# Smaller last chunks and a new place for the last value sums in a sparse graph-attention kernel

## Chip, core and metric

The kernel runs on one core of a Trainium2 chip. The metric is device time in microseconds (us) of one execution; lower is better. The engines are TensorE (PE in the profile), VectorE (DVE), ScalarE (ACT), GpSimd (POOL) and SyncE (SP).

## What is computed

The input is a matrix `x` of 3327 nodes with 256 features and an adjacency matrix with about 16 neighbours in each row. Layer 0 is a small graph attention; layers 1 to 3 are transformer layers whose attention is masked by the adjacency matrix:

```python
def layer(x, adj, ...):                      # layers 1, 2 and 3, 8 heads of 32
    q, k, v = split(layer_norm(x, g1, be1) @ w_qkv)
    scores = einsum('nhd,mhd->hnm', q, k) * HEAD_DIM ** -0.5
    attn = softmax(where(adj != 0, scores, -inf))
    x = x + einsum('hnm,mhd->nhd', attn, v) @ w_proj + b_proj
    h2 = layer_norm(x, g2, be2)
    return x + gelu(h2 @ w1 + b1) @ w2 + b2  # 256 -> 1024 -> 256
```

## The kernel before

Layer 0 also builds, for each node, the list of its neighbours. The nodes are sorted by their number of neighbours and cut into 26 blocks of 128. Block `b` has room for `CAPS[b]` neighbours: 40 for block 0, 24 for block 1, falling to 10 for block 25. Each of the layers 1 to 3 then works on gathered rows in place of a dense matrix.

**Groups.** The neighbours of a block are taken four at a time (`GS = 4`). A group is one tile `kv` with up to four rows of k and v for each of 128 nodes. It is filled by one indirect DMA for each neighbour, issued on GpSimd (L1226); ten such tiles are in a ring (`NBUF = 10`), and `issue()` for the next tile stands behind the step that frees one. There are 121 groups and 448 gathers in a layer.

**The order.** `ORDER` takes the blocks as 25, 1, 24, 2, ..., 14, 12, 13, and last block 0, the longest, with ten groups. In what follows K(b, s) is `scores` on the group of block `b` that starts at neighbour `s`: a product and a sum over each head on VectorE (L1248, L1249). V(b, s) is `values` on the same group: a product on VectorE (L1289, into one of three `vw` buffers) and two matmuls by the identity on TensorE, which the chip runs as four instructions (L1294), summed in the PSUM bank `po`. V follows K of the same block by roughly a block, since it needs the softmax.

**A turn.** `run()` goes through the groups in order. In each turn it does one K, then up to two V from `todo`, and then `some()`. A block's V may start when `wait` of the block is over 1, that is two turns after its last K. Two V are done in a turn when over five wait in `todo`, or when the block is block 0.

**Short steps.** After its last V a block puts nine steps on the list `short` (of which three are empty): copy and fold of `po`, a transpose (L1319), a copy, the projection (L1328, L1330), and `add` (L1334), which also takes the statistics of the second layer norm. `some()` takes one at its start and one at its end.

**Chunks and long steps.** Blocks are put together in chunks, by `CHUNK`: 3, 4, 4, 4, 4, 4, 2 and 1 blocks. When the last block of a chunk has been added, the chunk's steps are put on the list `long`: normalization (`scale`, 13 small VectorE instructions), transposes (L591), eight `up` matmul groups (L1373) with `gelu` on ScalarE (L1379), eight `down` groups (L1396, or L1389 for one block), the way back (L1402, L1410), the additions (L1414). In layers 1 and 2 there follow a second `scale`, transposes, and for each block `qkv` (L1426) and `keep` (L1432 to L1434), which writes the block's k and v rows for the next layer. In layer 3 there follows one `store` for each block (L1439), an indirect DMA on GpSimd. The next layer's first gather needs all `keep` writes of the layer.

**Pace.** Each long step has a cost. `some()` adds `rate` to `credit`, which is held to at most 8, and takes long steps while `credit` is over 0. For a chunk of four blocks the costs sum to 73.5 in layers 1 and 2, where two cost units of `up` or `down` are four matmul instructions with 512 columns. The rate is that sum over the number of groups in the next four blocks less two, about 16 turns, so 4.59. For the last chunk it is the sum over five.

**The end of a layer.** After the last K the remaining V are done one by one with `some()` in between, then `rate` is 4 and both lists are emptied.

The order within each engine is the order in which the program is written; the scheduler does not move instructions. So a step that waits holds up all that stands behind it on its engine.

Of the kernel before, what the change touches and what calls it, by code (L numbers as in the profile page):

```python
# [32 lines left out]
NB = (N + P - 1) // P  # L33
# [25 lines left out]
NBUF = 10  # L59

CB = 4
# [462 lines left out]
def sparse_path(ctx, tc, ins, out, dram, flag):  # L524
# [98 lines left out]
    with tc.tile_pool(name="a", bufs=1) as a, tc.tile_pool(name="aw", bufs=2) as aw, \  # L623
# [391 lines left out]
        def some(n):  # L1015
            for _ in range(n):
                if late:
                    late.pop(0)()
# [14 lines left out]
        for i in range(NB):  # L1033
# [8 lines left out]
            k = 1 if i < NB - 2 else 2  # L1042
# [147 lines left out]

    ORDER = [b for k in range(NB // 2) for b in (NB - 1 - k, k + 1)][:NB - 1] + [0]
    CHUNK, at = {}, 0
    for n in [CB - 1] + [CB] * ((NB - CB - 2) // CB) + [2, 1]:
        for b in ORDER[at:at + n]:
            CHUNK[b] = ORDER[at:at + n]
        at += n
    assert at == NB
    slots = {b: [(b, s) for s in range(0, CAPS[b], GS)] for b in ORDER}

    class Layer:  # L1200
# [101 lines left out]
        def block(self, b):  # L1302
            L, w, c = self.L, self.w, {}
            x = t2[:, b, :D]
            chunk = CHUNK[b]
            if b == chunk[0]:
                self.n2 = Norm(len(chunk), f"f{L}_{b}")
            n2 = self.n2

            def copy():  # L1310
                c["o"] = work.tile([P, D], FP, tag="o", name=f"o_{L}_{b}")
                nc.scalar.copy(c["o"], self.po[b][:, :D])

            def fold():
                nc.vector.tensor_add(c["o"], c["o"], self.po[b][:, D:])

            def turn():
                for k in range(2):
                    nc.tensor.transpose(self.po[b][:, k * P:(k + 1) * P],  # L1319
                                        c["o"][:, k * P:(k + 1) * P], ident)  # L1320

            def copy_T():
                c["oT"] = work.tile([P, 2 * P], FP, tag="oT", name=f"oT_{L}_{b}")
                nc.scalar.copy(c["oT"], self.po[b][:, :2 * P])

            def project():
                ps = self.po[b][:, D:]
                nc.tensor.matmul(ps, ones_bf[:96, :], bias3[:, 0, :], start=True, stop=False)  # L1328
                for k in range(2):
                    nc.tensor.matmul(ps, c["oT"][:, k * P:(k + 1) * P], w["w_proj"][:, k, :],  # L1330
                                     start=False, stop=(k == 1))

            def add():
                nc.vector.tensor_add(x, x, self.po.pop(b)[:, D:])  # L1334
                n2.stats(chunk.index(b), x)
                if b == chunk[-1]:
                    self.long += self.chunk(chunk, n2)
                    at = ORDER.index(b) + 1
                    turns = sum(len(slots[i]) for i in ORDER[at:at + CB])
                    turns = 5 if at == NB - 1 else turns - 2  # L1340
                    self.rate = sum(cost for cost, _ in self.long) / max(turns, 1)

            return [lambda: None, copy, lambda: None, fold, turn, copy_T, project, lambda: None, add]

# [133 lines left out]
        def some(self):  # L1478

            if self.short:  # L1480
                self.short.pop(0)()
            self.credit = min(self.credit + self.rate, 8.0)
            while self.long and self.credit > 0:
                cost, step = self.long.pop(0)
                self.credit -= cost
                step()
            if self.short:
                self.short.pop(0)()

        def run(self):  # L1490
            for _ in range(NBUF):
                self.issue()
            self.take_q(ORDER[0])

            todo, wait = [], {}

            def value():
                if todo[0][1] == 0:
                    self.weights(todo[0][0])
                self.values(*todo.pop(0))  # L1500

            for k, b in enumerate(ORDER):
                for g in slots[b]:
                    self.scores(*g)
                    if g == slots[b][-1]:
                        self.softmax(b)
                        if k + 1 < NB:
                            self.take_q(ORDER[k + 1])
                    for i in wait:
                        wait[i] += 1  # L1510
                    for _ in range(2 if len(todo) > NBUF // 2 or b == 0 else 1):
                        if todo and wait[todo[0][0]] > 1:
                            value()
                    self.some()
                todo += slots[b]
                wait[b] = 0
            while todo:
                value()
                self.some()
            self.rate = 4.0  # L1520
            while self.short or self.long:
                self.some()
# [45 lines left out]
```

## Time and profile before

| | |
|---|---|
| median of 10 runs | 2890.05 us (2876.18 to 2895.62) |
| the profiled execution | 2893.88 us |
| its span, first to last instruction | 2892.1 us |
| PE busy | 2005.4 us (69%) |
| DVE busy | 1981.1 us (69%) |
| POOL busy | 1359.2 us (47%) |
| ACT busy | 792.0 us (27%) |
| first gather of layers 1, 2, 3 | 634.2, 1414.7, 2187.5 us |
| last gather ends, layers 1, 2, 3 | 1293.2, 2067.5, 2797.0 us |

How to read it: busy shares are means over stages that differ. In each of the three layers there is a stretch with gathers (about 660, 653 and 610 us) and an end without (121 us from the last gather of layer 1 to the first of layer 2, 120 us from layer 2 to 3, and 95 us to the end of the span).

### The profile page before, as it was taken

The page shows a single profiled execution, that of the slowest core. Times are in us where ns is not written, and L with a number is a line of the kernel's source. Part 1 is how long each engine was busy: PE and PEld are TensorE (multiplying, and loading weights), DVE is VectorE, ACT ScalarE, POOL GpSimd, SP SyncE. Part 2 cuts the span into 40 slices and gives each one's busy share as a digit, 9 for nine tenths or more (in the row PEclk, how much of TensorE's full clock was granted, in tenths as well). Part 3 has the DMA queues.
Part 4 walks back from the last instruction along what each step waited for, and adds up shares of the span by engine and source line. Part 5 has one row for each costly group of instructions (what it writes and reads, how often), then busy time and mean ns, then how long its engine had stood idle before and what let it go on. Part 6 is the DMA issues. An engine that isn't in the chain of part 4 may idle for free. (4 is left out here: it accounts for less than half of the span.)

```text
span 2892.1 us, 21905 instructions
## 1 busy us (share of the span) xinstructions
PE 2005.4 (69%) x6391; PEld 1062.7 (37%) x6391; DVE 1981.1 (69%) x4141; ACT 792.0 (27%) x1363; POOL 1359.2 (47%) x1461
## 2 busy tenths in 40 slices
PE   4566666623778887787347878978782588777866
PEld 4444444411334333344213434434351243333334
DVE  2977787457787787773378876776724886778852
ACT  2443443200223332332102322322231023222221
POOL 3000000027775665650377656655405777777740
PEclk9677666756888988898678988988986799889988
DMA  4323321137776766660477656655506766666650
GB/s 178 135 97 113 125 105 55 50 116 218 217 222 186 203 203 181 187 179 16 138 209 210 194 176 176 193 168 153 135 26 184 210 201 195 188 190 189 204 136 15
DMA packets 144479, 453.67 MB, mean 157 GB/s; under 512 B 29521, under 2 KB 40156, under 8 KB 141021
## 3 DMA queue, kind: packets, MB, share of 16 engines
q0 software_dynamic: 113056, 370.26, 44.7%
q1 hardware_dynamic: 9834, 53.90, 5.2%
q10 hardware_dynamic: 21458, 28.02, 2.7%
q8 instruction: 52, 0.85, 0.1%
q14 instruction: 79, 0.65, 0.1%
HBM read 420.64 MB, written 31.42 MB: 156 GB/s over the span
## 5 line engine op out<-in xcount | busy, mean ns | idle before, releaser
L1226 POOL DMA_INDIRECT kv<-kv,t x1344 | 1273.3, 947 | 814.2 <-issue 355.4
L1294 PE MATMUL po<-vw,s_ident 128*128 128x512 f32 (+1 forms) x1380 | 773.1, 696 | 498.0 <-DVE vw L1289 450.1
L1248 DVE TENSOR_TENSOR kv<-kv,q 128x1024 f32<-128x1024 f32 (+3 forms) x363 | 413.2, 1138 | 311.0 <-ACT q L1234 153.6
L1294 PEld LDWEIGHTS po<-vw,s_ident 128*128 128x128 f32 x1380 | 284.7, 220 | 847.9 <-issue 470.8
L1249 DVE TENSOR_REDUCE sc<-kv 128x32 f32<-128x1024 f32 (+3 forms) x363 | 414.1, 1141 | 12.5
L1289 DVE TENSOR_TENSOR vw<-kv,w 128x1024 f32<-128x1024 f32 x333 | 371.2, 1127 | 0.2
L1373 PE MATMUL pu<-fT,s_w 128*128 128x512 f32 (+3 forms) x768 | 304.8, 531 | 1.0 <-ACT fT L596 1.0
L1396 PE MATMUL py<-gT,s_w 128*128 128x512 f32 (+2 forms) x672 | 282.9, 548 | 0.0
L1379 ACT ACTIVATE gT<-pu,pvb 128x512 f32<-128x512 f32 (+3 forms) x192 | 116.5, 608 | 355.6 <-PE pu L1373 355.3
L702 POOL MEMSET s_abf<- 128x1 bf16 x26 | 2.6, 103 | 434.9 <-PE s_ptb L714 252.0
L1373 PEld LDWEIGHTS pu<-fT,s_w 128*128 128x128 f32 x768 | 148.9, 203 | 138.6 <-issue 113.9
L1396 PEld LDWEIGHTS py<-gT,s_w 128*128 128x128 f32 x672 | 127.2, 191 | 122.3 <-issue 104.6
L714 PE MATMUL s_ptb<-s_ident_bf,s_abf 128*128 128x128 bf16 x676 | 76.6, 292 | 114.4 <-ACT s_aT L715 83.2
L724 DVE MAX8 cand<-s_v 128x8 f32<-128x208 bf16 x416 | 117.5, 359 | 0.9
L1426 PE MATMUL pk<-s_w_qkv,nT 128*128 128x512 f32 x208 | 110.1, 655 | 8.5 <-ACT nT L596 8.5
L714 PEld LDWEIGHTS <-s_abf 128*128 128x128 bf16 x676 | 65.4, 135 | 127.6 <-issue 93.5
L588 ACT ACTIVATE xn_f<-t,nm_f,rqy_f 128x256 f32<-128x256 f32 x78 | 42.9, 593 | 247.1 <-DVE nm_f L582 239.9
L1334 DVE TENSOR_TENSOR t<-t,po 128x256 f32<-128x256 f32 x78 | 32.5, 417 | 107.9 <-PE po L1330 104.0
L1263 ACT ACTIVATE sc<-sc,mx 128x120 f32<-128x120 f32 (+6 forms) x78 | 32.0, 410 | 259.5 <-DVE mx L1260 258.9
L715 ACT COPY s_aT<-s_ptb 128x896 bf16<-128x896 bf16 x104 | 83.3, 853 | 65.8 <-PE s_ptb L714 65.8
L1186 POOL DMA_INDIRECT t<-t,perm x26 | 24.6, 947 | 157.4 <-DMA colsb<-in_L_gnn_be_dram 149.8
L1414 DVE TENSOR_TENSOR t<-t,pd 128x256 f32<-128x256 f32 x75 | 29.5, 408 | 93.4 <-PE pd L1410 93.4
(285 smaller groups left out, 2458.3 us busy)
## 6 DMA issues: line engine op xcount, KB each, us to landing
s_a<-in_adj_dram SPq DMA_DIRECT2D x25, 1663.5 KB
kv<-kv,t POOLq DMA_INDIRECT x1344, 3.7
kv<-kvr ACTq DMA_DIRECT2D x52, 256.0 KB
kv<-s_kvr ACTq DMA_DIRECT2D x26, 256.0 KB
s_w<-in_L_gnn_w_dram SPq DMA_DIRECT2D x6, 1024.0 KB
t<-ql ACTq DMA_DIRECT2D x6, 592.0 KB
t<-s_x ACTq DMA_DIRECT2D x6, 512.0 KB
s_w_qkv<-in_L_gnn_w_qkv_dram SPq DMA_DIRECT2D x3, 768.0 KB
```

Of the source, the lines that this page charges most:

```text
L714: nc.tensor.transpose(pt[:, m, :], self.abf[:, k * P:(k + 1) * P], ident_bf)
L715: nc.scalar.copy(aT[:, k0:k0 + len(ks), :], pt[:, :len(ks), :])
L724: nc.vector.max(out=self.cand[:, s, :], in_=v[:, s, :])
L1226: nc.gpsimd.indirect_dma_start(out=t[:, s, :], out_offset=None, in_=kv[L], in_offset=bass.IndirectOffsetOnAxis(ap=t2[:, b, k:k + 1].bitcas ...
L1248: nc.vector.tensor_mul(k, k, self.q[b][:, None, :].to_broadcast([P, n, D]))
L1249: nc.vector.tensor_reduce(self.sc[b][:, s0:s0 + n, :], k.rearrange("p s (h d) -> p s h d", d=HD), AX.X, ALU.add)
L1289: nc.vector.tensor_mul(vw[:, :n * D].rearrange("p (s h d) -> p s h d", h=HEADS, d=HD), v, self.wp[b][:, s0:s0 + n, :, None].to_broadcast([ ...
L1294: nc.tensor.matmul(self.po[b][:, :m], ident, vw[:, s * D:s * D + m], start=(s0 + s == 0), stop=(s0 + s + 2 >= S), skip_group_check=True)
L1373: nc.tensor.matmul(c["pu", f][:, :n], w["w1"][:, e, f * P:(f + 1) * P], c["hT"][:, e, :n], start=(e == 0), stop=(e == 1))
L1379: nc.scalar.activation(g[:, :n], c.pop(("pu", f))[:, :n], AF.Gelu_apprx_tanh, bias=w["b1"][:, f:f + 1])
L1396: nc.tensor.matmul(c["py"][e][:, :n], w["w2"][:, f, e * P:(e + 1) * P], g[:, :n], start=(f == 0), stop=last)
L1426: nc.tensor.matmul(ps[:, :c1 - c0], c["hT"][:, e, j * P:(j + 1) * P], nxt["w_qkv"][:, e, c0:c1], start=(e == 0), stop=(e == 1))
```

## The change

Four edits, all in `CHUNK` and in the methods of `Layer`:

1. The chunks are 3, 4, 4, 4, 4, 2, 2, 2 and 1 blocks: blocks 10, 15, 11, 14, which were one chunk of four, become [10, 15] and [11, 14].
2. The rate is the sum of the waiting costs over 12 for a chunk of three or four blocks, and over 5 for a smaller one.
3. `some()` takes two short steps at its end instead of one when over eight wait, that is, right after a block's last V.
4. In the last two blocks of `ORDER` (13 and 0) two V are done in each turn and a block's V may start as soon as its softmax has been written; and after the last K all ten V of block 0 are done in one go, without `some()` in between.

```diff
-    for n in [CB - 1] + [CB] * ((NB - CB - 2) // CB) + [2, 1]:
+    for n in [CB - 1] + [CB] * 4 + [2, 2, 2, 1]:
...
-                    at = ORDER.index(b) + 1
-                    turns = sum(len(slots[i]) for i in ORDER[at:at + CB])
-                    turns = 5 if at == NB - 1 else turns - 2
-                    self.rate = sum(cost for cost, _ in self.long) / max(turns, 1)
+                    self.rate = sum(cost for cost, _ in self.long) / (12 if len(chunk) > 2 else 5)
...
-            if self.short:
-                self.short.pop(0)()
+            for _ in range(2 if len(self.short) > 8 else 1):
+                if self.short:
+                    self.short.pop(0)()
...
-                    for _ in range(2 if len(todo) > NBUF // 2 or b == 0 else 1):
-                        if todo and wait[todo[0][0]] > 1:
+                    last = k >= NB - 2
+                    for _ in range(2 if len(todo) > NBUF // 2 or last else 1):
+                        if todo and wait[todo[0][0]] > (not last):
                             value()
                     self.some()
...
             while todo:
                 value()
-                self.some()
```

## Prediction

> **What bounds the kernel now.** I read the busy time by stages first, since shares of the whole span hide that the stages differ. The columns are the stretch, its length, then busy us of PE, weight loads, DVE, ACT and POOL, the granted TensorE clock, the DMA share and GB/s. The first four rows go from K(11,0) of layer 1 to its last softmax and on to layer 2's first gather, and then the end of layer 3:
>
> ```profile
> 1149.00:1255.00 106.00, 86.23 (x216) 40.67 (x215) 76.71 (x135) 32.65 (x69) 64.07 (x69) 0.87 0.64 184
> 1255.00:1308.00 53.00, 45.57 (x117) 20.94 (x117) 39.18 (x63) 15.96 (x34) 29.07 (x31) 0.97 0.67 165
> 1308.00:1415.00 107.00, 74.05 (x249) 45.96 (x249) 31.49 (x104) 27.30 (x56) 0.34 (x1) 0.84 0.14 47
> ...
> 2806.00:2892.00 86.00, 55.94 (x192) 35.30 (x192) 25.39 (x64) 16.39 (x33) 7.07 (x7) 0.83 0.03 12
> ```
>
> Each layer ends with 86 to 107 us without gathers, in which TensorE works two thirds of the time. Next, one full cycle of a four-block chunk in the middle of layer 2 (turns K(9,4) to K(11,4), 103 us), cut at its stages: the FFN, then additions and second norm, then qkv:
>
> ```profile
> 1832.60:1877.50 44.90, 44.35 (x116) 20.76 (x115) 30.21 (x42) 19.54 (x29) 32.13 (x35) 0.97 0.68 200
> 1877.50:1897.90 20.40, 9.66 (x24) 3.93 (x22) 17.99 (x40) 2.56 (x5) 8.11 (x9) 0.73 0.44 130
> 1897.90:1911.80 13.90, 13.15 (x31) 6.97 (x32) 5.47 (x12) 4.64 (x8) 6.62 (x7) 0.66 0.52 152
> ```
>
> The bound alternates. In the FFN TensorE is never free and VectorE loses 44.9 - 30.2 = 14.7 us; in the additions VectorE is nearly full and TensorE idles; in qkv VectorE loses 8.4. Together they are the 23 us in which each cycle exceeds VectorE's own work.
>
> Layer 3 is another case. Its POOL rows show gathers back to back, 1.25 us apart, broken only by pairs of stores:
>
> ```profile
> 2558.39 0.94 POOL L1226 DMA_INDIRECT kv<-kv,t  x1 [0.30 <-issue]
> 2559.64 1.00 POOL L1439 DMA_INDIRECT out_dram<-t,perm  x1 [0.30 <-issue]
> 2563.26 0.98 POOL L1439 DMA_INDIRECT out_dram<-t,perm  x1 [2.62 <-DVE vw L1289]
> 2564.55 0.99 POOL L1226 DMA_INDIRECT kv<-kv,t  x1 [0.30 <-issue]
> ```
>
> 448 gathers x 1.25 = 560 of the 610 us from 2187.5 to 2797.0; a pair of stores adds 4.9 (2559.64 to 2564.55) in place of nothing. So layer 3's middle ends with GpSimd. The chain of waits of its last stretch:
>
> ```profile
> 2851.95 8.85 PE po L1294 x16
> 2861.22 0.43 DVE o L1315
> 2861.70 0.45 PE po L1319 x2
> 2862.87 0.88 PE po L1330 x4
> 2863.84 0.43 DVE t L1334
> ```
>
> The last V of block 0 end at 2860.8, 52 us after its softmax (2808.6), though ten V are 17.2 us of TensorE: chunk steps stand between them. From block 0's `add` (2863.85) to the end are 28.2 us, a chain with one block that the change leaves as it is.
>
> Prices on TensorE, from rows in order of time:
>
> ```profile
> 1852.60 1.88 PE L1373 MATMUL pu<-fT,s_w 128*128 128x512 f32 x4
> 1854.32 1.88 PE L1396 MATMUL py<-gT,s_w 128*128 128x512 f32 x4
> ```
> ```profile
> 1890.31 3.66 PE L1294 MATMUL po<-vw,s_ident 128*128 128x512 f32 x4 [4.79 <-DVE vw L1289]
> ```
> ```profile
> 2834.77 1.03 PE L1373 MATMUL pu<-fT,s_w 128*128 128x256 f32 x4
> 2835.63 1.03 PE L1396 MATMUL py<-gT,s_w 128*128 128x256 f32 x4
> ```
>
> Four instructions with 512 columns take 1.72 us (1852.60 to 1854.32), with 256 columns 0.86, and after an idle time of 4.8 us 3.66: a cold TensorE costs 1.9 more.
>
> **Layer 3's end.** Block 0's gathers end one store pair later, since [10, 15] now stores ahead of them: 2797.0 + 4.4 (net of the issue gap) = 2801.4, and the last K can start 2.8 us later (the lead that the gather-bound turns show), at 2804.2 against 2805.6 before. [12, 13] is normalized at K(0,28), so its FFN (16 x 0.86 = 13.8, with 1.7 for the cold start) is queued ahead of the V and done but for three steps at about 2815.6. The ten V follow in 17.2: 2832.8. Then those steps, the way back, two additions and two transposes stand between V and block 0's `add`: 6.7 us in place of 3.06, so `add` is at 2839.4 instead of 2863.85. Gain 24.5. If the V cannot start before the whole FFN and one more cold start, it is 16; if the FFN is done in time, 32. Cover: V hides behind nothing now, all 17.2 are on the path; they were there before too, with 35 us more between them.
>
> **Ends of layers 1 and 2**, in three legs from K(11,0), layer 1's row first.
> (i) To the last softmax. Before: 1148.7 to 1305.4, 156.7. After, three FFNs, [8], [10] and [11], and part of [12] must fit, where one and a half did. TensorE has 36 us of V, 10 of projections, 43 for [8] with its qkv, 43 for [10] and [11], 9 of [12]: 141; VectorE 130. Neither is the answer, as they take turns. Walking both queues with the durations above gives waits of VectorE of 7 to 14 us where an addition stands behind an FFN (block 10's, 11's, 12's `add` and the two chunks' additions), and the last softmax after 186, and 2.65 since `scale` of [8] now lies a turn earlier, ahead of K(11,0): 189, +32.
> (ii) From there to block 0's last V. Before: 1305.4 to 1381.2, 75.8. After: 12.5 until the FFN of [12] is through, 17.2 of V: 29.7, -46.
> (iii) To the next layer's first gather. Before: 33.5. After, the rest of [12] (additions 2.0, `scale` 2.6, transposes, qkv 5.2) is interleaved ahead of block 0's chain on each engine: 43, +9.5.
> Sum -4.6 in layer 1; in layer 2 (155.3, 75.9, 32.8 before) -2.7: -7 for both. Bounds for (i): 160, if TensorE's idle time there (27 of 157 us) takes the added work, and 205, with two more waits of 8: so -67 to +23 for both. The `keep` writes of [10, 15] and [11, 14] are issued on ScalarE's queue earlier than before and land long before the last one, which alone is waited for: 0.
>
> **The faster pace in the middle of layers 1 and 2.** Rate 6.12 for 4.59 does the FFN in about 6 turns instead of 8.5. TensorE, which bounds it, is rid of 2.5 x (1.72 for V + 0.36 for short steps) = 5.2; VectorE has 2.5 x 30.2/8.5 = 8.9 of turns left to do elsewhere: +3.7. In qkv, two blocks are now done in one turn, and the copy of q (L1234), which VectorE's next K needs, no longer stands behind a `keep`, which gives back 2.5. Net +1.2 a cycle; no row shows this pace, so from -3 (all of qkv's loss given back) to +7 (nothing given back, and two more cold V). There are 3.75 cycles in each layer (three full ones, and the first chunk of three blocks): +9 for both, from -22 to +52. In layer 3 it costs nothing: VectorE lags the gathers there by up to 5.7 us (leads of 8.5 against 2.8) and a V comes 4 us or more ahead of the gather that needs its tile; a lag 3 us longer is still covered. If not, 3 us a cycle, 12 in all, come on top.
>
> **The smaller edits.** Splitting a chunk adds one `scale` (2.65 us of VectorE) in each layer and a second one in layers 1 and 2; they are in the legs above. FFN with 256 columns costs half of 512, by the rows. The Trainium skill, page "TensorE: Matmul & The Clock Gate", section "Back-to-back issue gap", gives sustained spacings of 81 ns for 128 columns and 131 for 512, so narrow matmuls would cost more per column. Between the two, 256 columns would be near 98 (an estimate from that page), and the split FFN would take half as long again, some 14 us a layer more. The rows above disagree with it, and the sum goes by them. The two short steps after a last V bring a copy one turn forward: 0, under ScalarE's 27% load. Earlier V in block 13 free ring tiles earlier: 0, since GpSimd had the last gather out 9 us before its K in layer 1.
>
> **Sum.** -24.5 - 7 + 9 = -22.5. The profiled run was 2893.88 with a span of 2892.1; the median of the runs is 2890.05, 0.13% lower, and the difference is applied to it: 2867.5, taken as 2867.
>
> **Rivals.** A, the pace decides: bursts of FFN work make VectorE wait more than qkv gives back, +7 a cycle x 7.5 = 52, layer 3 gains 20, the ends nothing: 2922; with half of that cost and a layer-3 end of 16 it is still 2900. With the ends as forecast, it is slower from (24.5 + 7)/7.5 = 4.2 us a cycle on. For it: VectorE already loses 14.7 in the FFN; against it: the 8.4 lost in qkv are there to be had. 24%. B, the packed FFNs fit into TensorE's idle time: leg (i) is 170, so each end gains 23, the pace is free, layer 3 gains 25: 2890 - 46 - 25 = 2819. For it: 27 of 157 us idle in leg (i), 33 of 107 after it; against it: additions in VectorE's order behind each FFN. 15%. C, layer 3's gain is eaten by the pace and the ends (+20): within 0.2% of before. 9%. My forecast: 52%.
>
> A measurement of this kernel tells about 0.2% (6 us) from no change. Faster is the forecast and B: 67%; same C, 9%; slower A, 24%. The range reaches 2835 (much of B) and 2908 (the lower half of A).
>
> **What would show it.** Right: from layer 3's last K to the span's end about 63 us instead of 86; V of block 0 in one row of forty matmuls of some 17 us; K(9,4) to K(11,4) in layer 2 at 102 to 106; block 0's softmax in layer 1 later by some 30 and the next layer's first gather near 1415. Wrong: a cycle over 107 (rival A); that softmax less than 15 later (rival B); a POOL gap in layer 3's middle that ends with a VectorE V (lag not covered).

## The result, and the profile after

The changed kernel takes 2941.33 us (median of 8 runs, 2941.01 to 2947.17) against 2890.05 before: a ratio of 1.0186, with a 95% interval of 1.0173 to 1.0199. It is slower by 51 us, where the prediction was 2867 with a range up to 2908. The profiled execution has a span of 2940.1 us against 2892.1, so 48.0 us have to be found.

The simplest view is the length of each layer, and where in it the time is lost. All times are counted from the layer's first gather; the last two columns part each layer at K(11,0), which lies ahead of the last chunks.

| layer | length before | after | first gather to K(11,0), before | after | K(11,0) to the layer's end, before | after |
|---|---|---|---|---|---|---|
| 1 | 780.5 | 792.5 (+12.0) | 514.5 | 532.4 (+17.9) | 266.0 | 260.1 (-5.9) |
| 2 | 772.8 | 788.5 (+15.7) | 508.7 | 528.0 (+19.3) | 264.1 | 260.5 (-3.6) |
| 3 | 704.6 | 724.5 (+19.9) | 467.5 | 499.0 (+31.5) | 237.1 | 225.5 (-11.6) |

The ends, at which the split and the new place of V aim, became shorter, by 21 us in all. The middles, which the prediction had at +9, became longer by 69. The mark is not quite neutral: in the kernel after some 13 us of VectorE's work that lay behind K(11,0) now lie ahead of it (worked out below).

The ends look as forecast. The windows of the kernel after (columns: stretch, its length, busy us of PE, weight loads, DVE, ACT and POOL, clock, DMA share, GB/s) are, for layer 1, K(11,0) to the last softmax in two rows and on to layer 2's first gather, and last the end of layer 3 from the last K:

```profile
1167.00:1302.00 135.00, 107.92 (x320) 58.23 (x321) 88.32 (x176) 45.96 (x97) 76.39 (x81) 0.91 0.60 175
1302.00:1355.00 53.00, 38.08 (x129) 25.73 (x129) 35.48 (x66) 14.19 (x37) 15.11 (x16) 0.82 0.51 97
1355.00:1427.00 72.00, 54.20 (x190) 34.64 (x189) 25.13 (x69) 18.89 (x40) 0.00 (x0) 0.90 0.17 55
2874.00:2940.00 66.00, 46.33 (x168) 31.53 (x168) 22.07 (x45) 13.16 (x28) 2.91 (x3) 0.84 0.02 8
```

The stretch from the last softmax to the next layer's first gather, 109 us before, is 72, and the one ahead of it, from K(11,0), is 188 in place of 157. TensorE is busy for three quarters of the 72 us, where it was for two thirds. In the timeline, V of block 0 in layer 3 stand in one row of forty instructions, and block 0's `add` comes 6 us after it:

```profile
2887.17 1.03 PE L1393 MATMUL py<-gT,s_w 128*128 128x256 f32 x4
...
2888.03 17.33 PE L1294 MATMUL po<-vw,s_ident 128*128 128x512 f32 x40
...
2911.52 0.42 DVE L1334 TENSOR_TENSOR t<-t,po 128x256 f32<-128x256 f32 x1 [2.20 <-PE po L1330]
```

In the middle of layer 3 the picture is new. Where pairs of stores stood alone between gathers that ran 1.25 us apart, GpSimd now waits for a ring tile, does six gathers, and then three stores in a row, which wait for each other (POOL's timeline):

```profile
2580.12 0.94 POOL L1226 DMA_INDIRECT kv<-kv,t  x1 [2.28 <-DVE vw L1289]
...
2587.62 1.00 POOL L1436 DMA_INDIRECT out_dram<-t,perm  x1 [0.30 <-issue]
2590.71 0.98 POOL L1436 DMA_INDIRECT out_dram<-t,perm  x1 [2.09 <-DMA out_dram<-t,perm]
2593.40 0.97 POOL L1436 DMA_INDIRECT out_dram<-t,perm  x1 [1.71 <-DMA out_dram<-t,perm]
2594.68 0.99 POOL L1226 DMA_INDIRECT kv<-kv,t  x1 [0.30 <-DVE mx L1260]
```

The second place where the profile changed is one group of VectorE, block `add` (L1334). Its row on the page of before, and of after (the part after the bar: busy us, mean ns, then the idle time ahead of it and its releaser):

```profile
L1334 DVE TENSOR_TENSOR t<-t,po 128x256 f32<-128x256 f32 x78 | 32.5, 417 | 107.9 <-PE po L1330 104.0
```
```profile
L1334 DVE TENSOR_TENSOR t<-t,po 128x256 f32<-128x256 f32 x78 | 32.7, 419 | 243.1 <-PE po L1330 210.5
```

VectorE waits 135 us more ahead of this `add`, 106 of them for the projection of a block. At the same time its idle time ahead of K (L1248) falls from 311.0 to 164.4 us, most of it the wait for q (153.6 to 66.8). So the waits have changed places; this row says where to look, and not how much was lost.

### The profile page after: what moved, and what is told of

Its sections match the earlier page's. It is cut to its first block, busy times and chain, and to the rows that moved or that the text cites. A ratio compares the mean times of both kernels' runs of the same rounds, so it can differ in the third digit from the quotient of the medians.

```text
span 2940.1 us, 22461 instructions
## 1 busy us (share of the span) xinstructions
PE 2003.0 (68%) x6583; PEld 1102.4 (37%) x6583; DVE 1994.8 (68%) x4206; ACT 772.3 (26%) x1379; POOL 1358.6 (46%) x1461
## 4 chain that ended last, share of the span: by engine, by line
PE 22%; DVE 12%; DMA 8%; POOL 7%; issue 7%; ACT 1%; DVEq 0%; POOLq 0%; ACTq 0%
PE po L1294 8%; DMA kv<-kv,t 8%; POOL kv L1226 7%; PE pu L1370 5%; PE py L1393 4%; DVE kv L1248 3%; DVE vw L1289 3%; DVE sc L1249 2%; PE pk L1423 1%; PE po L1330 1%; PE pq L1423 0%; PE py L1386 0%; DVE t L1334 0%; DVE t L1411 0%; POOL out_dram L1436 0%
## 5 line engine op out<-in xcount | busy, mean ns | idle before, releaser
L1294 PE MATMUL po<-vw,s_ident 128*128 128x512 f32 (+1 forms) x1380 | 756.7, 686 | 459.6 <-DVE vw L1289 459.4
L1248 DVE TENSOR_TENSOR kv<-kv,q 128x1024 f32<-128x1024 f32 (+3 forms) x363 | 412.7, 1137 | 164.4 <-DMA kv<-kv,t 88.3
L1370 PE MATMUL pu<-fT,s_w 128*128 128x512 f32 (+3 forms) x864 | 314.0, 499 | 5.4 <-ACT fT L596 4.9
L1370 PEld LDWEIGHTS pu<-fT,s_w 128*128 128x128 f32 x864 | 169.6, 206 | 122.7 <-issue 87.8
L1334 DVE TENSOR_TENSOR t<-t,po 128x256 f32<-128x256 f32 x78 | 32.7, 419 | 243.1 <-PE po L1330 210.5
L1393 PEld LDWEIGHTS py<-gT,s_w 128*128 128x128 f32 x768 | 144.8, 190 | 97.2 <-issue 73.8
L1324 ACT COPY oT<-po 128x256 f32<-128x256 f32 x78 | 28.9, 370 | 349.6 <-PE po L1319 339.1
L591 PE MATMUL pf<-s_ident,xn_f 128*128 128x128 f32 x156 | 40.8, 378 | 86.2 <-ACT xn_f L588 85.1
```

The lines of the kernel that those rows point to most:

```text
L1248: nc.vector.tensor_mul(k, k, self.q[b][:, None, :].to_broadcast([P, n, D]))
L1294: nc.tensor.matmul(self.po[b][:, :m], ident, vw[:, s * D:s * D + m], start=(s0 + s == 0), stop=(s0 + s + 2 >= S), skip_group_check=True)
L1370: nc.tensor.matmul(c["pu", f][:, :n], w["w1"][:, e, f * P:(f + 1) * P], c["hT"][:, e, :n], start=(e == 0), stop=(e == 1))
L1393: nc.tensor.matmul(c["py"][e][:, :n], w["w2"][:, f, e * P:(e + 1) * P], g[:, :n], start=(f == 0), stop=last)
```

## Experiments

The first theory, P, was that the faster pace is the loss; its rival, S, that the split of the last chunks and the new place of V are. The experiments fell on two kinds of chip. On the first kind the kernel before takes 2890 to 2895 us, on the second 3404 to 3419, with nearly the same work done; each run is compared with the kernel before on its own chip, and a finding of the second kind was tried again on the first where it mattered. e1 to e12 ran on the second kind, e13 to e18 on the first. ("Kind" is only a name for the two levels of time: at least two chips were met at each.)

### The parts one by one, second kind of chip

`e1_pace_back`: the kernel after, with the old pace for chunks of more than two blocks.

```diff
-   self.rate = sum(cost for cost, _ in self.long) / (12 if len(chunk) > 2 else 5)
+   at = ORDER.index(b) + 1
+   turns = sum(len(slots[i]) for i in ORDER[at:at + CB]) - 2
+   self.rate = sum(cost for cost, _ in self.long) / (turns if len(chunk) > 2 else 5)
```

Expected: 

> The changed kernel with the pace of the kernel before for chunks of three or four blocks (sum of the costs over the groups of the next four blocks less two); chunks of two and one stay at five turns, the last V stay in one go. Mark: time from a layer's first gather to its K(11,0); before 508.7 us in layer 2 and 467.5 in layer 3, with the change 528.0 and 499.1. Theory P (the faster pace is what costs): the marks go back to 509 to 513 and 468 to 475, and the time falls by 15 + 15 + 28 us from 2941 to about 2880 to 2890. Theory S (the split of the last chunks and the place of the last V cost it, and the pace only shifts work that is given back at the end): the time stays within 10 us of 2941.

Measured: 3373.19 us, ratio 0.9902 (0.9874 to 0.9931).

`e2_pace_only`: the kernel before with the new rate alone.

```diff
-   turns = 5 if at == NB - 1 else turns - 2
-   self.rate = sum(cost for cost, _ in self.long) / max(turns, 1)
+   self.rate = sum(cost for cost, _ in self.long) / (12 if len(chunk) > 2 else 5)
```

Expected: 

> The kernel before with the faster pace alone (sum over 12 for chunks of three or four, over 5 for smaller). Theory P: the marks to K(11,0) are those of the change (528 and 499), and since the fifth chunk of four runs at this pace too, the time is 2890 + 17 + 17 + 30 = 2954, from 2935 to 2965. Theory S: 2890 to 2900.

Measured: 3462.71 us, ratio 1.0178 (1.0146 to 1.0210).

`e3_values_only`: the kernel before with the new rule for V in the last two blocks and V of block 0 in one go.

```diff
-   for _ in range(2 if len(todo) > NBUF // 2 or b == 0 else 1):
-       if todo and wait[todo[0][0]] > 1:
+   last = k >= NB - 2
+   for _ in range(2 if len(todo) > NBUF // 2 or last else 1):
+       if todo and wait[todo[0][0]] > (not last):
...
    while todo:
        value()
-       self.some()
```

Expected: 

> The kernel before with the V part alone: two V in each turn of the last two blocks, V right after the softmax, all ten V of block 0 in one go. Both theories leave the marks to K(11,0) as before (508.7 and 467.5). What is asked is the end of a layer: the last V end 30 us or less after the last softmax instead of 76, but the rest of chunk [10, 15, 11, 14] and chunk [12, 13] then stand behind them and ahead of block 0's own chunk. TensorE's work after the softmax is the same 74 us either way, so the time should be 2890 within 12 us under P; under S it is slower by 15 or more.

Measured: 3355.69 us, ratio 0.9849 (0.9821 to 0.9876).

`e4_split_only`: the kernel before with the new chunks alone.

```diff
-   for n in [CB - 1] + [CB] * ((NB - CB - 2) // CB) + [2, 1]:
+   for n in [CB - 1] + [CB] * 4 + [2, 2, 2, 1]:
```

Expected: 

> The kernel before with the split of chunk [10, 15, 11, 14] alone, pace and V as before. Chunk [8, 17, 9, 16] is then half done when [10, 15] is queued. Theory P: the marks to K(11,0) stay; the ends change by little, 2880 to 2900. Theory S: one more normalization in each layer and FFN work packed ahead of VectorE's additions cost 10 to 15 us a layer: 2915 to 2935.

Measured: 3413.66 us, ratio 1.0031 (1.0014 to 1.0049).

What follows, for this kind of chip: the pace by itself is a loss, the new rule for V with V in one go a gain that was larger than P had allowed for (P had it within 12 us), the split a small loss, 0.3%, and with the old pace the change as a whole is a gain. This looked like a clean case for P. The three parts multiply to 1.0055, though, and the kernel after has 1.0186 on the first chip; so the kernel after was run here too.

### Is it layer 3, and is it the ring?

`e8_after_again`: the kernel after, unchanged.

Expected: 

> The kernel after, unchanged, beside the others on the same chip: 1.0186 of the kernel before if this chip is like the first one. If it is the one on which the first four experiments ran, their factors multiply (1.0178 x 0.9849 x 1.0031) to 1.0055, while e1_pace_back with the pace's own factor gives 1.0078: 1.004 to 1.010.

Measured: 3458.79 us, ratio 1.0124 (1.0096 to 1.0152). More than the parts give: something is missing from the list.

`e5_fast_l12`: the kernel after, with the old pace in layer 3.

```diff
+   turns = 12 if self.L < 3 else turns
+   self.rate = sum(cost for cost, _ in self.long) / (turns if len(chunk) > 2 else 5)
```

Expected: 

> The kernel after, with the old pace (about 16 turns) for chunks of four in layer 3 alone; layers 1 and 2 keep the 12 turns. Theory P (the fast pace is the cost, and it costs in every layer): layer 3 carries most of it, since its gathers wait for late V and for bunched stores; the gathers of layer 3 lose their lines 'kv <- DVE vw', and the time falls to 0.985 to 0.988 of the kernel after. Rival Q (in layer 3 VectorE's lag is covered and the stores, not the pace, hold the gathers): within 0.3% of the kernel after, so the loss lies in layers 1 and 2.

Measured: 3457.49 us, ratio 1.0107 (1.0078 to 1.0136), so 0.9996 of e8 (0.996 to 1.004, from the two intervals). P's expectation missed: on this kind of chip layer 3 loses nothing by the pace. Gathers are not its bound there: 448 of them at 1.25 us are 560 of the layer's 888 us in e8, and POOL's waits for V sum to 173 us in e8 and 166 in e5.

`e7_early_v_l3`: the kernel after, with V of every block of layer 3 allowed one turn earlier.

```diff
-   if todo and wait[todo[0][0]] > (not last):
+   if todo and wait[todo[0][0]] > (not (last or self.L == 3)):
```

Expected: 

> The kernel after, with V of each block in layer 3 allowed a turn earlier (as soon as the softmax is written), so that each ring tile comes free about 5 us earlier at the fast pace. If the gathers' waits for tiles (47 us of 'kv <- DVE vw' in layer 3 of the kernel after) are a loss by themselves: 0.985 to 0.99 of the kernel after, and these lines shrink below 15 us. If the FFN bursts delay VectorE anyway and the waits only show that: within 0.4% of the kernel after, and K(0,0) of layer 3 no more than 10 us earlier.

Measured: 3441.91 us, ratio 1.0083 (1.0046 to 1.0121), so 0.995 of e8 (0.990 to 1.000, from the two intervals). K(0,0) of layer 3 is 2.5 us earlier and the waits for V are 165.6 us in place of 173.4. The first expectation, that they shrink below 15 us, missed; the time lies just outside the 0.4% of the second, and its interval reaches both. Since the edit hardly shortened the waits, it does not tell what they cost.

### Can the parts be put together?

`e6_values_slow`: e3 with a pace slower than before's, about 19 turns.

```diff
-   turns = 5 if at == NB - 1 else turns - 2
+   turns = 5 if at == NB - 1 else turns + 1
```

Expected: 

> The kernel before with V of block 0 in one go and two V a turn in the last two blocks (as e3_values_only), and a slower pace: the sum over the groups of the next four blocks plus one (about 19 turns) in place of less two (about 16). Theory P, if slower goes on to be better: 0.970 to 0.980 of the kernel before, below the 0.985 of e3_values_only. Rival R (the old pace is at its best, since a chunk's FFN must be through before the next chunk is ready): 0.985 to 1.0, with what is left over at the end of a layer showing as a longer stretch from the last K to the next layer's first gather.

Measured: 3341.07 us, ratio 0.9762 (0.9730 to 0.9794). Slower goes on to be better, as P said.

`e9_before_again`: the kernel before, for its trace on this kind of chip.

Expected: 

> The kernel before, unchanged, for its trace beside the experiments: 3400 to 3425 us, since the kernel before took 3404 and 3419 in the two comparisons so far. It gives the layers' lengths by which the parts of the change can be told apart: theory P wants layers 1 and 2 longer in e2_pace_only than here by 20 us each, and layer 3 of e4_split_only longer than here by 20 or more if the two small bursts of the split cost most there.

Measured: 3421.74 us; its layers take 970.3, 938.8 and 875.7 us. e2's take 969.8, 955.9 and 888.6, e4's 973.3, 938.9 and 881.7: of the differences named in the expectation, layer 2 of e2 is longer by 17.1 us, near the 20 of P, but layer 1 is not longer, and layer 3 of e4 is longer by 6.0 and not by 20. On these chips a layer's length can't be read from one execution: e5 and e8 have the same program in layers 1 and 2 and differ by 11.0 us in the one and by 17.7 the other way in the other.

`e10_best`: put together from such readings, the split in layers 1 and 2 alone, the slow pace there alone, and e3's rules for V.

```diff
+   for n in [CB - 1] + [CB] * 4 + ([2, 2, 2, 1] if L < 3 else [CB, 2, 1]):
...
+   turns = 5 if len(chunk) < 3 else turns + 1 if self.L < 3 else turns - 2
```

Expected: 

> Made from the parts that were a gain: V of block 0 in one go and two V a turn in the last two blocks, the split of [10, 15] and [11, 14] in layers 1 and 2 alone, the slower pace (19 turns) in layers 1 and 2 alone. Theory P with the split's loss in layer 3: the layers' lengths of the experiments (split against none: 16 and 24 us shorter in layers 1 and 2, 57 longer in layer 3; slow pace: 8 and 16 shorter in layers 1 and 2, 17 longer in layer 3) sum to 0.963 to 0.973 of the kernel before. If single profiles mislead on the layers: 0.976 to 0.985, no better than e6_values_slow.

Measured: 3364.97 us, ratio 0.9850 (0.9820 to 0.9880). No better than e3: single profiles had misled on the layers.

### The mechanism of the pace

`e11_half_old` and `e12_half_fast`: half of the FFN's matmuls are left out, at the old pace and at the fast one.

```diff
-   for e in range(2):
-       nc.tensor.matmul(c["pu", f][:, :n], w["w1"][:, e, f * P:(f + 1) * P],
-                        c["hT"][:, e, :n], start=(e == 0), stop=(e == 1))
+   nc.tensor.matmul(c["pu", f][:, :n], w["w1"][:, 0, f * P:(f + 1) * P],
+                    c["hT"][:, 0, :n], start=True, stop=True)
...
+   if f % 2:            # in down()
+       return
```

Expected of the first: 

> The kernel before with half of the FFN's matmuls left out (up over one half of its contraction, down for every second group; gelu, copies, additions and all else stay). It is the base of e12_half_fast: 0.955 to 0.985 of the kernel before, since some 290 us of TensorE go, most of it beside other work.

Expected of the second: 

> The kernel of e11_half_old (half of the FFN's matmuls left out) at the fast pace (12 turns). Theory P in its narrow form (at the fast pace TensorE's FFN work in a turn exceeds VectorE's turn, and VectorE waits for it): with half the matmuls the burst fits into the turn, and the time is within 0.5% of e11_half_old. Rival V (it is the bunching of the small steps on VectorE, ScalarE and the queues, whatever TensorE does): 1.012 to 1.018 of e11_half_old, as at full size.

Measured: 3311.77 us (3305.29 to 3314.19), ratio 0.9682 (0.9656 to 0.9708), and 3298.46 us (3288.11 to 3305.76), ratio 0.9646 (0.9611 to 0.9682). The fast pace takes 0.9960 of the time of the old one (3298.46 / 3311.77; 0.992 to 1.001 from the two intervals), where with the whole FFN it took 1.0178. All the small steps are still bunched as at full size. So what the fast pace costs on this kind of chip is TensorE's FFN work in a turn, and not the bunching.

### The other kind of chip

`e14_slow_only`: the kernel before with the slower pace alone (the line of e6).

Expected: 

> The kernel before with the slower pace alone (19 turns in place of 16). If pace and place of the last V are independent (0.9762 / 0.9849): 0.988 to 0.994 of the kernel before. If the slower pace pays only with V in one go, since otherwise the last chunks' steps lie between the last V: 0.998 to 1.005.

Measured: 2856.83 us, ratio 0.9869 (0.9847 to 0.9891). The slow pace pays by itself, a little more than the first expectation had it.

`e13_values_slower`: as e6, with `turns + 5`.

Expected: 

> As e6_values_slow, with a pace slower still: the groups of the next four blocks plus five (about 23 turns). Theory P as a trend (1.8% from 16 to 12 turns, 0.9% from 19 to 16): 0.966 to 0.974 of the kernel before. Rival R: a chunk is no longer through when the next one is ready, what is left over runs into the layer's end, and the best pace lies between: 0.977 to 0.990.

Measured: 2878.54 us, ratio 0.9944 (0.9924 to 0.9964). Rival R had the direction, and the time lies above its range. The middle hardly gains any more: K(11,0) comes 7.8 and 3.2 us earlier than in e18 below in layers 1 and 2 and 3.3 later in layer 3, and 4 to 5 us of VectorE's work in layers 1 and 2 have only moved behind it. The end gives back more (last K to the next layer's first gather 129.4 against 113.5 in layer 1).

`e15_one_go_only`: the kernel before, with the one `some()` after the last K left out.

```diff
    while todo:
        value()
-       self.some()
```

Expected: 

> The kernel before with one line left out: the ten V of block 0 after the last K are done without some() between them. By the prediction's terms for the ends (24.5 us in layer 3 and 7 in the others, of which the split had a part): 0.988 to 0.993 of the kernel before, and the two V a turn in blocks 13 and 0 give the rest of the 0.985 of e3_values_only. Rival: the early V of the last two blocks are the gain of e3_values_only: 0.996 to 1.003.

Measured: 2883.70 us, ratio 0.9975 (0.9959 to 0.9990): within the rival's range. In layer 3 the V end 29.3 us earlier (644.0 for 673.3 us after the first gather) and the layer 2.4 earlier: without the split, the chunk steps that stood between the V now stand behind them. That the early V make up the rest of e3's gain was not run by itself on this kind of chip.

`e16_split12_slow`: e10 with the slow pace in layer 3 too.

```diff
-   turns = 5 if len(chunk) < 3 else turns + 1 if self.L < 3 else turns - 2
+   turns = 5 if len(chunk) < 3 else turns + 1
```

Expected: 

> e10_best with the slower pace in layer 3 too, that is e6_values_slow plus the split of [10, 15] and [11, 14] in layers 1 and 2. If e10_best lost to e6_values_slow by the faster pace in layer 3: 0.970 to 0.978 of the kernel before. If the split is the loss (as e4_split_only's 1.0031 says): 0.981 to 0.988.

Measured: 2853.85 us, ratio 0.9853 (0.9832 to 0.9874). The second expectation held: with the split there is less gain than without it (e18 below).

`e17_pace_again`: the kernel of e2 on this kind of chip.

Expected: 

> The kernel of e2_pace_only (the kernel before with the fast pace alone) once more, since chips differ: theory P says 1.012 to 1.022 of the kernel before on a chip of the first kind too, with K(11,0) of layer 3 later by 20 to 32 us as in the kernel after. Rival: the pace is the loss only where engines stall for instructions anyway, and on a chip of the first kind it is within 0.5% of the kernel before; the loss of the kernel after would then come from the split.

Measured: 2909.46 us, ratio 1.0054 (1.0037 to 1.0072). Between the two: the pace is a loss here too, of 16 us and not of 51. **So theory P, that the pace is the whole loss, falls on the kind of chip on which the loss was measured.**

`e18_values_slow_again`: the kernel of e6 on this kind of chip.

Expected: 

> The kernel of e6_values_slow once more, for the same reason. On a chip of the first kind: the slower pace alone gave 0.9869 and V in one go alone 0.9975, with the split 0.9853; the parts multiply to about 0.984. Expected 0.976 to 0.986; if V early in the last two blocks costs on such a chip: 0.986 to 0.992.

Measured: 2818.79 us, ratio 0.9743 (0.9724 to 0.9762). A little better than expected; this version beats both kernels.

### What the traces of the first kind of chip add

On this kind of chip one trace repeats another well. Up to K(11,0) the programs of e14, e16 and e18 are the same (their other edits act later), and K(11,0) comes 494.0, 493.4 and 494.8 us after the first gather in layer 1, 485.6, 488.2 and 485.1 in layer 2, 466.5, 466.3 and 466.2 in layer 3: within about 3 us. That lets pairs of traces be read as experiments.

**The pace.** One row of windows for each of four kernels, layer 2 from K(5,0) to K(9,0), two cycles of chunks. In order: 12 turns (e17), 16 (before), 19 (e14), 23 (e13).

```profile
1620.70:1830.80 210.10, 167.78 (x432) 78.84 (x432) 153.92 (x266) 56.37 (x100) 125.74 (x134) 0.89 0.60 176
```
```profile
1614.30:1820.20 205.90, 171.41 (x435) 80.71 (x433) 154.50 (x265) 62.02 (x105) 125.63 (x134) 0.88 0.61 181
```
```profile
1583.80:1778.10 194.30, 157.93 (x425) 76.88 (x424) 153.73 (x266) 55.12 (x98) 127.62 (x136) 0.89 0.65 192
```
```profile
1595.70:1784.50 188.80, 162.98 (x431) 79.11 (x431) 150.98 (x250) 57.36 (x99) 127.78 (x136) 0.92 0.67 198
```

VectorE's busy time stays near 154 us; its idle time (length less busy) is 56.2, 51.4, 40.6 and 37.8. The slower the FFN is handed out, the less VectorE waits behind it, which agrees with e11 and e12. (The last row has 16 VectorE instructions fewer, so part of its gain is work that has moved on.) From 16 to 12 turns a cycle costs 2.1 us, from 16 to 19 it gains 5.8. Up to K(11,0) the kernel before and e17 do the same work, and e17 comes 8.0, 7.9 and 14.7 us later in the three layers. From K(11,0) to the layer's end it is 3.9, 4.7 and 7.8 us shorter, so of these 30.6 us the faster pace gives 16.4 back by itself.

**The fourth part.** Up to K(11,0) the kernel after and e17 differ by one edit alone, the two short steps after a block's last V: the first five chunks are the same, the pace is the same, and the rule for V acts in the last two blocks. Yet K(11,0) comes later in the kernel after: 532.4 against 522.5 us in layer 1, 528.0 against 516.6 in layer 2, 499.0 against 482.2 in layer 3, so by 9.9, 11.4 and 16.8. Of this, 4.5, 4.7 and 4.0 us are work that now lies ahead of K(11,0), one more `add` and one more `scale`; the rest, 25 us in three layers, is waiting. The rows for layer 2 from the first gather to K(11,0), e17 and then the kernel after (VectorE's busy time is the third entry behind the length):

```profile
1419.10:1935.70 516.60, 363.21 (x921) 170.69 (x921) 382.16 (x624) 116.75 (x215) 333.37 (x352) 0.84 0.63 186
```
```profile
1427.10:1955.10 528.00, 364.90 (x930) 173.58 (x930) 386.82 (x640) 117.48 (x216) 336.73 (x356) 0.85 0.62 184
```

The figure depends a little on the mark: at K(15,0), one block earlier, the kernel after is 25.2 us behind in the three layers, and 20 of them are waiting. The waits of VectorE in one window of layer 2 (1600 to 1960 us; line, what it waited for, us, times, longest), in the kernel after and in e17:

```profile
DVE t L1334 <- PE po L1330: 32.8, 10, 9.2
DVE o L1315 <- ACT o L1312: 19.6, 9, 4.7
DVE kv L1248 <- ACT q L1234: 16.6, 5, 4.1
DVE t L1334 <- ACT q L1234: 8.4, 1, 8.4
DVE t L1411 <- PE pd L1407: 4.8, 5, 2.3
DVE t L1334 <- PE pn L591: 1.4, 1, 1.4
```
```profile
DVE kv L1248 <- ACT q L1234: 43.8, 7, 9.7
DVE t L1411 <- PE pd L1407: 23.8, 6, 7.8
DVE o L1315 <- ACT o L1312: 12.8, 7, 3.3
DVE t L1334 <- PE po L1330: 0.2, 1, 0.2
```

The two lists sum to 83.6 and 80.6 us: the waits have above all changed places, and what is left of them is small. In the two cycles from K(5,0) to K(9,0) VectorE idles 57.0 us in the kernel after and 56.2 in e17:

```profile
1633.90:1849.00 215.10, 168.81 (x439) 80.88 (x437) 158.11 (x280) 56.80 (x101) 127.65 (x136) 0.89 0.59 175
```

The edit does more than bring one copy forward, and it does not act after every last V. `some()` takes a step at its start, so the nine new steps are only eight when they are counted, unless a step of the block before still waits. Up to K(11,0) that is so in ten turns of a layer, at every second block or so (1, 2, 3, 4, 21, 20, 19, 18, 17, 16). Each time all steps behind it come earlier, also those of the blocks that follow. For block 17, `copy` comes from the start of a turn to the end of the turn but one before, behind that turn's FFN steps, and the projection and `add` come from a turn's end to a turn's start. For block 8, which the next rows show, every short step keeps its place in the turn and comes one turn earlier. Block 18's `add` comes a turn earlier too, and with it the FFN of its chunk, so block 8's `copy`, which in e17 stands ahead of the FFN, now stands behind its first steps. The timeline of the kernel after shows both new waits in one cycle:

```profile
1860.99 0.69 ACT L1376 ACTIVATE gT<-pu,pvb 128x512 f32<-128x512 f32 x1 [1.03 <-PE pu L1370]
...
1861.58 0.36 ACT L1312 COPY o<-po 128x256 f32<-128x256 f32 x1
...
1861.97 0.42 DVE L1315 TENSOR_TENSOR o<-o,po 128x256 f32<-128x256 f32 x1 [4.22 <-ACT o L1312]
...
1876.46 1.88 PE L1393 MATMUL py<-gT,s_w 128*128 128x512 f32 x4
...
1878.18 1.88 PE L1294 MATMUL po<-vw,s_ident 128*128 128x512 f32 x4
...
1880.01 1.03 PE L1330 MATMUL po<-s_w_proj,oT 128*128 128x256 f32 x4
...
1881.14 0.42 DVE L1334 TENSOR_TENSOR t<-t,po 128x256 f32<-128x256 f32 x1 [9.19 <-PE po L1330]
```

`copy` waits on ScalarE behind two `gelu`, which wait for TensorE, and `fold` on VectorE waits 4.2 us for it. Then VectorE reaches `add` while TensorE still works through the FFN that stands ahead of the projection: 9.2 us. In e17 the same FFN costs VectorE 8.2 us at the next K, which waits for q, and the `add` behind that K waits for 0.3:

```profile
1862.36 1.22 DVE L1248 TENSOR_TENSOR kv<-kv,q 128x1024 f32<-128x1024 f32 x1 [8.17 <-ACT q L1234]
...
1864.02 1.03 PE L1330 MATMUL po<-s_w_proj,oT 128*128 128x256 f32 x4
...
1865.08 0.42 DVE L1334 TENSOR_TENSOR t<-t,po 128x256 f32<-128x256 f32 x1 [0.25 <-PE po L1330]
```

Not all of this stays lost: counted from layer 2's first gather, VectorE's idle time is 13.1 us more than e17's at K(16,0), and 5.3 more at K(15,0). The edit was not run by itself; that it is the cause rests on this pair of programs and the three layers that agree, and the share of each of the shifted steps stays open. For the second kind of chip the ratios allow an estimate, if the parts multiply: e1 is 1.002 of what e3 and e4 multiply to (0.998 to 1.007, from the intervals), so with the old pace the edit may cost nothing, and e8 is 1.007 of e2, e3 and e4 (1.002 to 1.012).

**Layer 3.** POOL's waits from 2260 to 2730 us, which holds most of the layer's gathers, in the kernel before, in e17 and in the kernel after:

```profile
POOL out_dram L1439 <- DMA out_dram<-t,perm: 12.4, 5, 3.9
...
POOL kv L1226 <- DVE vw L1289: 2.4, 8, 0.3
```
```profile
POOL out_dram L1436 <- DMA out_dram<-t,perm: 21.8, 8, 8.5
...
POOL kv L1226 <- DVE vw L1289: 9.9, 12, 1.8
```
```profile
POOL kv L1226 <- DVE vw L1289: 24.9, 12, 6.2
POOL out_dram L1436 <- DMA out_dram<-t,perm: 21.3, 8, 8.3
```

The pace brings the stores closer together, so that they wait for each other (+9.4 us), and makes V late for the ring (+7.5); the short steps make V later still (+15.0). The sizes are near what K(11,0) lost: 14.7 by the pace and 16.8 by the short steps, 4.0 of these moved work. That GpSimd's waits are the cause there is argued from this; no run shows it.

**The split.** e16 against e18, that is the split in layers 1 and 2 (with its small chunks over five turns) at the slow pace, is 0.9853 against 0.9743. From K(11,0) to the layer's end it costs 17.5 us in layer 1 (270.9 against 253.4) and 17.4 in layer 2 (269.6 against 252.2): the last K comes 46.2 us later in layer 1 (186.1 against 139.9 us after K(11,0)), and the rest of the end is 28.7 shorter. **V in one go with two V a turn**, e18 against e14, gains 8.4, 14.7 and 11.4 us in the three layers.

**The two together, at the fast pace.** From K(11,0) to the layer's end the kernel after is 2.0 us shorter than e17 in layer 1, 1.1 longer in layer 2 and 3.8 shorter in layer 3, though 13.2 us of VectorE's work lie ahead of the mark already. So against e17 the three edits gain nothing behind K(11,0): with that work put back they cost 8.5 us. How much of this is the split, the V or the short steps was not run on this kind of chip.

## Why the prediction was wrong

By its own steps, with the traces of the first kind of chip:

| step | predicted us | measured us, and from which pair |
|---|---|---|
| pace, layers 1 and 2 | +9 (-22 to +52) | +15.9 at K(11,0), e17 against before |
| pace, layer 3 | 0 (12 if not covered) | +14.7 at K(11,0), same pair |
| two short steps | 0 | +38.1 at K(11,0), after against e17 (9.9, 11.4, 16.8): 24.9 waiting, 13.2 work that lay behind it |
| ends of layers 1 and 2 | -7 | -9.5, after against before, from K(11,0); -0.3 with the moved work put back |
| end of layer 3 | -24.5 | -11.6, after against before, from K(11,0); -7.6 with the moved work put back |
| sum | -22.5 | +47.6, and 0.4 ahead of layer 1 |

**The step that failed most is the one that was given one sentence.** "The two short steps after a last V bring a copy one turn forward: 0, under ScalarE's 27% load." In its place stand 25 us of waiting, the largest miss of any term, though not the largest loss: the pace costs 30.6 us up to the same mark, of which 9 were forecast. Two things are wrong in the sentence. It looked at the step that moves first and not at those behind it, of which one, `add`, is where VectorE meets TensorE and, at a chunk's last block, sets the chunk's FFN going; and it took ScalarE's load over the whole span as cover, where what counts is what stands ahead in the queue at that place: `gelu` steps that wait for TensorE. The change was also described as acting right after every last V; by the order of the steps it acts only where a step of the block before is left.

**The pace.** The price in layers 1 and 2 was near: 2.1 us a cycle in e17 against 1.2, inside the range given. What was wrong was "in layer 3 it costs nothing". The prediction gave VectorE's lag as covered if it grew by 3 us, and 12 us as the price if not; it cost 14.7. The sign that it had named, a gap of GpSimd that ends with a VectorE V, is what the kernel after shows. Most of these gaps come with the short steps (24.9 us against 9.9 in e17). It had not seen that stores which come closer together wait for each other.

**The ends of layers 1 and 2** came out near what was worked: in layer 1, with VectorE's last softmax step as the mark, 187.8 us from K(11,0) against 189, 30.0 to the last V against 29.7, 42.3 to the next gather against 43. This walk through both queues, instruction by instruction, was the part with the most work in it, and the only one that came within about a microsecond. Part of that is luck: the walk counted the `scale` that moves ahead of K(11,0) (2.65 us) as a cost of the leg, and of the 4.5 us of VectorE's work that moved, the `add` was not foreseen. The sum of legs also hid what the edits in it do apart. The pace alone, e17, shortens the two ends by 8.6 us of the 9.5; by e16 and e18, at the slow pace, the split costs 17 us a layer, and by e14 and e18 the V gain 8 and 15. A better kernel lay close by: the new rule for V without the split, at a slower pace. (The bounds of the forecast for these ends, redone from the legs, are -65 to +25 in place of -67 to +23; nothing rests on the difference.)

**Layer 3's end** was nearly right from the last K on: 65.9 us against the forecast 63 (86.5 before). Ahead of it, K(11,0) to the last K became 9.0 us longer (159.6 against 150.6), where the prediction had the last K come 1.4 earlier. The two bursts of the split chunks are the likely reason, since the pace alone makes this stretch shorter (145.0 in e17); no run has them alone in this layer. That the gain behind the last K needs the FFN of [12, 13] to be ahead of the V is suggested by e15, where V in one go, without the other edits, gains 2.4 in the layer.

**The small matmuls** cost half for half the columns, as the rows had said: in the kernel after, groups of four with 256 columns start 0.86 us apart.

```profile
2878.36 1.03 PE L1393 MATMUL py<-gT,s_w 128*128 128x256 f32 x4
2879.22 1.03 PE L1370 MATMUL pu<-fT,s_w 128*128 128x256 f32 x4
```

The Trainium skill, page "TensorE: Matmul & The Clock Gate", section "Back-to-back issue gap", also has a formula for a single matmul's gap, columns over 2.4 GHz plus 2.5 ns, so 109 ns for 256 columns and 216 for 512 (an estimate from that page). The rows have 215 and 430 ns for one instruction (0.86 and 1.72 us for four), close to twice that; why twice, no run here shows. The sustained figures of the same section, which would have made narrow matmuls dearer, do not describe this stream.

**The rivals.** Rival A had the right side, and its point of decision held: the cycles of the kernel after between K(5,0) and K(9,0) take 107.8 us in layer 1 and 107.6 in layer 2, 4.9 and 4.6 more than before, over its 4.2. Its mechanism was the larger part of the waiting in these cycles: VectorE's idle time in the two cycles is 50.1 us before, 54.9 in e17 and 57.0 after in layer 1, and 51.4, 56.2 and 57.0 in layer 2; the rest, 1.4 and 1.8 us a cycle, is VectorE's work that moved into the window. But the pace was not the larger part of the kernel's loss, as e17 shows. The cycle named as a sign, K(9,4) to K(11,4) in layer 2, took 105.8 and would have passed as "right": one cycle was too small a sample. Rival B was wrong in its reason, as TensorE's idle time did not take the added FFN.

The last experiments also correct the first reading of this study. On the second kind of chip the pace alone had the whole loss (1.0178 against 1.0124 for the kernel after), and a run on the first kind (1.0054) was needed to see that there it has a third of it. The three other edits together are a gain beside the pace on the second kind (1.0124 against 1.0178) and a loss on the first (1.0186 against 1.0054); why they differ stays open.

## What to carry to other kernels

When a list of steps is handed out by position in a loop, moving one step moves all behind it; walk each of them through the queue that it now stands in, above all the one where two engines meet. A pace for background work wants to be the slowest that is through in time: a burst that fills one engine makes the other wait, and here a slower pace gained 1.3% by itself, until, at a slower one still, the leftovers ran into the layer's end. Edits that meet in one diff should be priced apart even where their sum is right, and tried on the chip that the number is for.

## What was not expected of the hardware

The two kinds of chip differ by 18% on the same program, with nearly the same busy times (the kernel after: PE 2094.8 us in e8 and 2003.0 on the first kind, DVE 1994.6 and 1994.8; the granted clock is 0.773 and 0.819). Up to the first gather of layer 1 both take 634 to 636 us; all of the difference lies behind it. There, engines of the second kind stand idle where no recorded event ends the wait. Waits of the kernel before on the second kind (e9), VectorE's and TensorE's:

```profile
DVE t L1334 <- remote: 159.3, 15, 15.6
```
```profile
PE po L1294 <- issue: 198.6, 49, 35.2
```

Neither line is among the waits on the first kind. What causes them was not found. Stores of layer 3 issued directly after one another start 2.7 to 3.1 us apart, against 1.25 for gathers: each waits for the one before it, and bunched stores cost GpSimd that time.
